# A transformer block on one core: the feed-forward's steps reordered within a slot, small columns given rings of their own, the last pair put first

## The chip, the cores and the metric

The kernel runs on one core of a Trainium2 chip. The core has a matrix engine (TensorE, "PE" in the profile, with its weight loads shown apart as "PEld"), a vector engine (VectorE, "DVE"), an activation engine (ScalarE, "ACT"), a general engine (GpSimd, "POOL") and a queue that here issues most transfers (SyncE, "SP"). Each works through its own instructions in order and they meet at semaphores. The metric is device time of one execution in microseconds (us); lower is better.

## What is computed

Sixteen sequences of 224 tokens with 512 features pass through a gated cross-attention and a gated feed-forward network with quantised activations and ternary weights. The context of a sequence has 750 rows, and a mask says which of them the softmax keeps. Cut to what matters:

```python
def xattn(x, context, mask):                       # 8 heads of 64
    q, k, v = x @ W_q, context @ W_k, context @ W_v          # split into heads
    sim = einsum('bihd,bjhd->bhij', q, k) * 64 ** -0.5
    sim = where(mask[:, None, None, :], sim, -finfo.max)
    return einsum('bhij,bjhd->bihd', softmax(sim), v).reshape(b, n, 512) @ W_o + b_o

def act_quant(x):                                  # to 8 bits, by row
    scale = 127.0 / clip(max(abs(x), axis=-1), 1e-5)
    return clip(round(x * scale), -128, 127) / scale

def weight_quant(w):                               # to -1, 0, 1
    scale = 1.0 / clip(mean(abs(w)), 1e-5)
    return clip(round(w * scale), -1, 1) / scale

def bitlinear(x, w, b):
    return einsum('bsd,fd->bsf', act_quant(rmsnorm(x)), weight_quant(w)) + b

def ffn(x):                                        # 512 -> 2048 -> 512
    return bitlinear(gelu(bitlinear(x, w1, b1)), w2, b2)

x = x + tanh(g_xattn) * xattn(layernorm(x), ctx, mask)
x = x + tanh(g_ffn) * ffn(layernorm(x))
```

## The kernel before, in words

**Two tilings.** Attention goes by *slots*: the 16 batches are sorted by how many context rows the mask leaves them, only those rows are gathered, and slot s handles the s-th batch with room for 192 rows (slots 0 to 7, called wide here) or 128 (slots 8 to 15, narrow). The feed-forward goes by *tiles* of 128 tokens, two of them making a *pair*: 28 tiles, 14 pairs. Tokens of all slots lie one after another, 224 to a slot, so a pair of 256 tokens begins in one slot and ends in the next.

**Attention of a slot.** `scores` (line 1037) makes one of four units of `sim`, takes off the mask's part and the row maximum on VectorE (L1061), the exponential on ScalarE (L1071), the reciprocal of the sum (`rec`, L1080), and multiplies the probabilities `p` by it on GpSimd (L1081). `turn_probs` (L1091) transposes them on TensorE (`ptp`, `ptr`), `weighted` (L1115) multiplies by the values (`av`) and stores the result transposed in `xoT`. Beside it run the steps for the next slot: `context_pieces` (`ctxp`, `kp`, `vp`, `vr`), `query_pieces` (`xnp`, `qp`) and `norm_pieces`.

**Feed-forward of a pair.**
- `residual(i)` (L1175) fetches the pair's rows of x into `y` by two indirect transfers on GpSimd's queue (L793) and adds the output bias there (L1182). `y` has three buffers.
- `project(i, k)` (L1184) multiplies `xoT` by `w_o` (`op`, L1189, eight matmuls for a tile as counted in the profile) and adds it to `y` on VectorE (L1192).
- `normalise(i)` (L1213) does layernorm and the first quantisation on VectorE, from the statistics (L1226) to the cast of `xq` (L1236), and transposes `xq` into `xqT` by a DMA from the SP queue (L1237). GpSimd works out the factor `c1` and adds the second bias to `y` (L1242 to L1247).
- `up(i, k, g)` (L1250) makes one half of the 2048 hidden columns of a tile (`hp`, L1259, eight matmuls) and evicts it with factor and bias on VectorE into `h` (L1267).
- `gelu(i, ks)` (L1272) applies the activation on ScalarE (L1279), takes the row's largest absolute value (L1282), quantises and casts to `hq` on VectorE (L1285, L1286), transposes it by a DMA from SP into `hqT` (L1288), and squares `h` on ScalarE for the row's norm (L1290), from which GpSimd makes the factor `c2` (L1292, L780, L1208 to L1210).
- `down(i, k)` (L1300) multiplies `hqT` by the second weights (`fp`, L1304, 16 matmuls), adds to `y` on VectorE (L1308), and scatters the tile to the output by an indirect transfer on GpSimd's queue (L1310).

**What sets the order.** In each slot the main loop (L1505 on) makes three streams: attention, the next slot's preparation, and `flow`, the feed-forward. Each is a list of pieces with a cost. `merge` (L1434) always takes the next piece of the stream that has done the smallest share of its own total cost, so a piece stands at a share of the slot. Before, `flow` is

```python
flow: residual(p); up(p-1), gelu(p-1); project(p), normalise(p); down(p-1)
```

`project` of a pair needs its 256 tokens complete, which holds in every slot from 2 on but slot 9. So slot 9 has only an up, slot 10 no up, slot 2 only a project. After the last slot come project and normalise of pair 13, up(12), then up(13) woven with down(12), then down(13).

The framework (Tile) is given this program order as priorities, and places each engine's instructions by a model of when their inputs are ready: an instruction that the model sees ready may go ahead of an earlier one that it sees waiting, and `tc.high_priority()` puts what is inside ahead of the rest. It also puts in all the waits, those for buffers among them. A tile's tag names its ring, and `bufs` how many buffers the ring has. Small columns of 2, 4 and 6 floats come from three rings (`small`, L782, of 24, 6 and 6 buffers), whatever they hold; `fx` of `normalise` and `hq` of `gelu` share a ring of three buffers. Results of TensorE wait for eviction in four small buffers (`gen`) and two of twice the size (`wide`, used by `sim`, `hp` and `av`).

Of the kernel before, what the change touches and what calls it, by code (L numbers as in the profile page):

```python
# [16 lines left out]
EPS = 1e-5  # L17
# [708 lines left out]
def compact_path(ctx, tc, sh, x, context, out, late_loads):  # L726
# [54 lines left out]

    def small(name, n=2):  # L782
        return pa.tile([P, n], F32, tag=f"s{n}", name=name, bufs=24 if n == 2 else 6)

# [159 lines left out]
    def norm(i, ks=(0, 1)):  # L944

        xp = normed[i]
        name = f"x{i}_{ks[0]}"
        part = slice(ks[0], ks[-1] + 1)
        mv = small(f"mv_{name}", 4).rearrange("p (k n) -> p k n", k=2)
        for k in ks:  # L950
            st = small(f"bs_{name}_{k}", 6)
# [3 lines left out]
        rstd = small(f"rs_{name}")  # L955
        nc.gpsimd.tensor_scalar(rstd[:, part], mv[:, part, 1], 1.0, EPS, ALU.mult, ALU.add)
        pow_half(rstd[:, part])
        less = small(f"ls_{name}")
        nc.gpsimd.tensor_scalar(less[:, part], mv[:, part, 0], -1.0, 0.0, ALU.mult, ALU.add)
        for k in ks:  # L960
            nc.gpsimd.tensor_scalar(
                xp[:, k, :], xp[:, k, :], less[:, k : k + 1], rstd[:, k : k + 1], ALU.add, ALU.mult
            )

    def norm_first(k):

        xp = normed[0]
        st = small(f"bs_x0_{k}", 6)
        nc.vector.bn_stats(st, xp[:, k, :])
        mv = small(f"mv_x0_{k}", 4)  # L970
        nc.vector.bn_aggr(mv[:, :2], st)
        rstd = small(f"rs_x0_{k}")
# [64 lines left out]
    def scores(s, n):  # L1037
# [16 lines left out]
        probs = pa.tile([TQ, 4, 192], F32, tag="p", name=f"p_{s}_{n}", bufs=3)  # L1054
        total = small(f"sum_{s}_{n}", 4)
        for i in range(2):
            for j in range(2):
# [20 lines left out]
                )  # L1078
        rec = small(f"rec_{s}_{n}", 4)
        nc.vector.reciprocal(rec[:TQ], total[:TQ])  # L1080
# [117 lines left out]
    def quantiser(amax, part, least, name):  # L1198
        k = small(f"k_{name}")
        nc.vector.tensor_scalar(k[:, part], amax[:, part], least, 1.0 / 127.0, ALU.max, ALU.mult)  # L1200
        nc.vector.reciprocal(k[:, part], k[:, part])
        load["v"] += 300
        return k

    def unquantiser(amax, r, part, isw, name):

        c = small(f"c_{name}")
        nc.gpsimd.tensor_tensor(c[:, part], amax[:, part], r[:, part], ALU.mult)  # L1208
        nc.gpsimd.tensor_scalar(c[:, part], c[:, part], 1e-5, None, ALU.max)
        nc.gpsimd.tensor_scalar(c[:, part], c[:, part], isw, None, ALU.mult)  # L1210
        return c

    def normalise(i, ks=(0, 1)):  # L1213
# [3 lines left out]
        part = slice(ks[0], ks[-1] + 1)  # L1217
        mv = small(f"mv_y{name}", 4).rearrange("p (k n) -> p k n", k=2)
        if ks[0] == 0:
            f["fx"] = late["rows"].tile([P, 2, D], F32, tag="hq", name=f"fx_{i}", bufs=3)  # L1220
            f["xq"] = pa.tile([P, 2, D], BF16, tag="xq", name=f"xq_{i}", bufs=3)
            f["xqT"] = pa.tile([P, 2 * ND, P], BF16, tag="xq", name=f"xqT_{i}", bufs=3)
        fx, xq, xqT = f["fx"], f["xq"], f["xqT"]
        for k in ks:
            st = small(f"bs_y{name}_{k}", 6)
# [3 lines left out]
        amax = small(f"a1_{name}")  # L1229
        nc.vector.tensor_reduce(amax[:, part], fx[:, part, :], AX.X, ALU.max, apply_absolute_value=True)  # L1230
# [9 lines left out]

        r = small(f"r1_{name}")
        nc.gpsimd.tensor_scalar(r[:, part], mv[:, part, 1], 1.0 + EPS, EPS * EPS, ALU.mult, ALU.add)  # L1242
# [29 lines left out]
    def gelu(i, ks=(0, 1)):  # L1272
        f = pairs[i]
        name = f"{i}_{ks[0]}"
        part = slice(ks[0], ks[-1] + 1)
        ss = small(f"ss_{name}")
        amax = small(f"a2_{name}")
        for k in ks:
            nc.scalar.activation(f["h", k], f["h", k], AF.Gelu)  # L1279
        for k in ks:  # L1280
            h = f["h", k]
            nc.vector.tensor_reduce(amax[:, k : k + 1], h, AX.X, ALU.max, apply_absolute_value=True)  # L1282
            scale = quantiser(amax, slice(k, k + 1), 1e-5 * EPS**0.5, f"2_{i}_{k}")
            hq = late["rows"].tile([P, FF], BF16, tag="hq", name=f"hq_{i}_{k}", bufs=3)
            nc.vector.tensor_scalar(hq.bitcast(I16), h, scale[:, k : k + 1], None, ALU.mult)  # L1285
            nc.vector.tensor_copy(hq, hq.bitcast(I16))  # L1286
# [4 lines left out]
        r = small(f"r2_{name}")  # L1291
        nc.gpsimd.tensor_scalar(r[:, part], ss[:, part], 1.0 / FF, EPS, ALU.mult, ALU.add)  # L1292
# [4 lines left out]
        load["v"] += len(ks) * (2282 + 1280 + 690)  # L1297
        load["s"] += len(ks) * 2 * 1910 + 2600

    def down(i, k):  # L1300
# [70 lines left out]
    def scale_weights(wi):  # L1371
        tot = small(f"wtot_{wi}")
# [3 lines left out]
        mean = small(f"wmean_{wi}")  # L1376
        nc.vector.tensor_scalar(mean[:, 0:1], pt, 1.0 / (FF * D), 1e-5, ALU.mult, ALU.max)
# [127 lines left out]
    for s in range(B):  # L1505
# [10 lines left out]
        else:  # L1516
# [4 lines left out]
            if complete:  # L1521
                flow.append((0.0, lambda i=projected: residual(i)))
            if raised < projected:
                flow += up_pieces(raised)
                raised += 1
            if complete:
                flow += project_pieces(projected)
                projected += 1
                if lowered < raised:
                    flow += down_pieces(lowered)  # L1530
                    lowered += 1
        merge(attention_pieces(s), other, flow)
# [8 lines left out]
    i = NPAIR - 1  # L1541
    residual(i)
    for k in range(2):
        project(i, k)
        normalise(i, (k,))
    downs = down_pieces(i - 1) + down_pieces(i)
    for _, piece in up_pieces(i - 1):
        piece()
    for _, piece in weave(up_pieces(i), downs[:2]) + downs[2:]:
        piece()  # L1550
# [34 lines left out]
```

## Time and profile before

| what | us |
|---|---|
| median of 6 runs (753.59 to 761.06) | 759.87 |
| the profiled execution | 759.97 |
| its span, first to last instruction | 758.1 |
| slots 3 to 7 (wide), 147.7 to 391.8 | 46.7 to 50.3 each |
| slots 8, 11 to 14, from one slot's first `sim` to the next | 39.2 to 40.9 each |
| slots 9 and 10 | 29.1 and 32.2 |
| slot 15, up to the first vector work on the last `op` | 653.55 to 692.85 |
| from there to the end of the span | 65.3 |

The profile shows one execution. An engine's busy time is the sum of what its instructions took. "A <- B" in the waits says that A's engine stood idle and what B it waited for last, with the total, the number of times and the longest. A line such as L1259 is a line of the kernel. The granted clock is the share of TensorE's full clock that the throttle allowed in a stretch. The weights of the feed-forward are loaded and rounded in slots 0 and 1, before any feed-forward work; the last `y` is followed by its transfer and the program's closing.

### The profile page before, as it was taken

The numbers are of one execution on the slowest core, as the hardware profiler recorded it, in microseconds if no ns is written. First come the engines' busy times: TensorE is split into PE (matmuls) and PEld (weight loads), VectorE is DVE, ScalarE is ACT, GpSimd is POOL, SyncE is SP. The second block draws the span as 40 slices with busy tenths as digits, with TensorE's granted clock in tenths as the row PEclk, the third lists the DMA queues.
The fourth block names the chain that finished last, engine by engine and source line by source line (L and its number), as shares of the span: only waits on it lengthen the run. The fifth ranks groups of instructions, "written<-read, shape, count | busy, mean of one in ns | idle before, by whom it ended". The sixth has DMA issues, their size and how long they took to land.

```text
span 758.1 us, 11378 instructions
## 1 busy us (share of the span) xinstructions
PE 685.4 (90%) x3902; PEld 437.1 (58%) x3902; DVE 505.6 (67%) x1300; ACT 407.7 (54%) x960; POOL 398.3 (53%) x543
## 2 busy tenths in 40 slices
PE   4997799999999999998999999999999999889652
PEld 3875587666566666555656575666666566443221
DVE  5499756876584674664758676588584939495860
ACT  1547565384663855736647368365565656460530
POOL 6583567464554644647266564575654454535141
PEclk9999899999999999999999999999999999999877
DMA  5884021132223322222142323123131222222250
GB/s 193 312 265 155 21 80 45 15 72 56 70 44 70 85 51 57 67 57 81 28 98 67 70 67 67 42 68 82 54 64 62 57 69 57 70 43 62 41 106 31
DMA packets 87218, 58.77 MB, mean 78 GB/s; under 512 B 75488, under 2 KB 75632, under 8 KB 87024
## 3 DMA queue, kind: packets, MB, share of 16 engines
q1 hardware_dynamic: 79024, 32.00, 18.8%
q0 software_dynamic: 8128, 25.96, 10.7%
q8 instruction: 33, 0.54, 0.3%
q14 instruction: 33, 0.27, 0.1%
HBM read 32.26 MB, written 7.34 MB: 52 GB/s over the span
## 4 chain that ended last, share of the span: by engine, by line
PE 58%; DVE 14%; issue 10%; POOL 9%; DMA 4%; ACT 3%; POOLq 0%; DVEq 0%; ACTq 0%; SPq 0%
PE qp L1008 9%; PE op L1189 9%; PE fp L1304 8%; PE hp L1259 7%; PE kp L892 5%; PE sim L1047 4%; PE vp L907 4%; PE ptp L1101 3%; DVE a L1282 3%; PE av L1126 3%; DVE h L1267 2%; POOL p L1081 2%; DMA hqT<-hq 2%; DVE hq L1285 2%; DVE p L1061 1%
## 5 line engine op out<-in xcount | busy, mean ns | idle before, releaser
L1081 POOL TENSOR_TENSOR p<-p,rec 112x768 f32<-112x768 f32 (+1 forms) x64 | 84.2, 1318 | 76.8 <-DVE rec L1080 43.9
L1304 PE MATMUL fp<-w2T,hqT 128*128 128x512 fp8e4 x448 | 106.7, 394 | 14.8 <-DMA hqT<-hq 14.8
L1259 PE MATMUL hp<-w1T,xqT 128*128 128x512 fp8e4 x448 | 107.4, 384 | 8.2 <-DVE h L1267 5.4
L1071 ACT ACTIVATE p<-p,nm 112x192 f32<-112x192 f32 (+1 forms) x256 | 106.4, 419 | 11.6 <-DVE nm L1061 11.4
L1008 PE MATMUL qp<-xnT,wq_sb 128*128 128x224 f32 x512 | 105.6, 360 | 0.6 <-ACT xnT L766 0.6
L1189 PE MATMUL op<-wo_sb,xoT 128*128 128x512 f32 x224 | 103.7, 599 | 0.0
L1008 PEld LDWEIGHTS qp<-xnT,wq_sb 128*128 128x128 f32 x512 | 97.4, 194 | 6.5 <-issue 3.6
L1267 DVE SCALAR_TENSOR_TENSOR h<-hp,c,b_bc 128x1024 f32<-128x1024 f32 x56 | 71.6, 1280 | 41.1 <-PE hp L1259 38.6
L1061 DVE CUSTOM_DVE_ANT_0 p<-sim,mask 112x192 f32<-112x192 f32 (+1 forms) x256 | 67.7, 319 | 34.2 <-PE sim L1047 32.7
L1304 PEld LDWEIGHTS <-hqT 128*128 128x128 bf16 x448 | 44.0, 101 | 73.6 <-DMA hqT<-hq 17.7
L1282 DVE TENSOR_REDUCE a<-h 128x1 f32<-128x2048 f32 x28 | 63.9, 2282 | 21.5 <-ACT h L1279 21.2
L1259 PEld LDWEIGHTS <-xqT 128*128 128x128 bf16 x448 | 43.5, 98 | 57.2 <-issue 15.2
L1308 DVE SCALAR_TENSOR_TENSOR y<-fp,c,y 128x512 f32<-128x512 f32 x28 | 20.9, 746 | 80.0 <-PE fp L1304 80.0
L1310 POOL DMA_INDIRECT out_dram<-y,token x28 | 30.9, 1104 | 78.2 <-DVE y L1308 74.0
L1290 ACT ACTIVATE h<-h 128x2048 f32<-128x2048 f32 x28 | 53.4, 1908 | 22.3 <-DVE hq L1285 14.9
L1279 ACT ACTIVATE h<-h 128x2048 f32<-128x2048 f32 x28 | 53.5, 1910 | 19.6 <-DVE k L1200 11.2
L1189 PEld LDWEIGHTS op<-wo_sb,xoT 128*128 128x128 f32 x224 | 40.6, 190 | 38.9 <-issue 36.4
L892 PE MATMUL kp<-ctxT,wk_sb 128*128 128x192 f32 (+1 forms) x384 | 63.0, 313 | 0.0
L892 PEld LDWEIGHTS kp<-ctxT,wk_sb 128*128 128x128 f32 x384 | 57.6, 198 | 6.4 <-issue 4.5
L1247 POOL TENSOR_TENSOR y<-y,b_bc 128x512 f32<-128x512 f32 x28 | 36.6, 1311 | 38.7 <-DVE fx L1228 38.4
L766 ACT COPY pT<-ptp 128x448 f32<-128x448 f32 x63 | 32.7, 536 | 40.3 <-PE ptp L1101 40.1
L1047 PE MATMUL sim<-kT,qT 64*112 64x192 f32 (+1 forms) x512 | 51.4, 316 | 1.1 <-DVE h L1267 1.0
(165 smaller groups left out, 1177.3 us busy)
## 6 DMA issues: line engine op xcount, KB each, us to landing
raw<-in_L_ffn_w_dram SPq DMA_DIRECT2D x16, 512.0 KB, 6.2
wq_sb<-in_L_xattn_W_q_dram SPq DMA_DIRECT2D x1, 1024.0 KB, 5.6
b_bc<-in_L_ffn_b_dram SPq DMA_DIRECT2D x1, 1024.0 KB, 9.5
wk_sb<-in_L_xattn_W_k_dram SPq DMA_DIRECT2D x1, 768.0 KB, 7.2
wv_sb<-in_L_xattn_W_v_dram SPq DMA_DIRECT2D x1, 768.0 KB, 8.6
wo_sb<-in_L_xattn_W_o_dram SPq DMA_DIRECT2D x1, 512.0 KB, 3.6
wo_sb<-in_L_xattn_W_o_dram SPq DMA_DIRECT2D x2, 256.0 KB, 6.6
x<-in_x_dram,token POOLq DMA_INDIRECT x28, 3.6
```

Of the source, the lines that this page charges most:

```text
L892: nc.tensor.matmul(pk[:, p - p0, :], lhsT=sh.wk[:, c, p * P : (p + 1) * P], rhs=st["ctxT"][:, c, :cap], start=(c == 0), stop=(c == NC - 1),)
L1008: nc.tensor.matmul(pq[:, i, :], lhsT=sh.wq[:, d, (p + i) * P : (p + i + 1) * P], rhs=st["xnT"][:, d, :], start=(d == 0), stop=(d == ND - 1),)
L1047: nc.tensor.matmul(sim[:, j, i, :cap], lhsT=st["qT"][j * DH : (j + 1) * DH, p, q * TQ : (q + 1) * TQ], rhs=st["kT"][j * DH : (j + 1) * DH, ...
L1061: nc.vector.tensor_tensor_reduce(out=probs[:, h, :cap], in0=sim[:, j, i, :cap], in1=st["mask"][:, j * begin : j * begin + cap], scale=-(DH ...
L1071: nc.scalar.activation(probs[:, h, :cap], probs[:, h, :cap], AF.Exp, bias=nmax, scale=-1.0, accum_out=total[:TQ, h : h + 1],)
L1081: nc.gpsimd.tensor_tensor(probs[:, :, :cap], probs[:, :, :cap], rec[:TQ].unsqueeze(2).to_broadcast([TQ, 4, cap]), ALU.mult,)
L1189: nc.tensor.matmul(po, lhsT=xoT[:, d, at : at + P], rhs=sh.wo[:, d, :], start=(d == 0), stop=(d == ND - 1))
L1259: nc.tensor.matmul(ph[:, n, :], lhsT=f["xqT"][:, k * ND + d, :], rhs=w1T[:, d, at : at + NB], start=(d == 0), stop=(d == ND - 1),)
L1267: nc.vector.scalar_tensor_tensor(h[:, cols], ph.rearrange("t i n -> t (i n)"), f["c1", k], sh.b1[:, cols], ALU.mult, ALU.add)
L1279: nc.scalar.activation(f["h", k], f["h", k], AF.Gelu)
L1282: nc.vector.tensor_reduce(amax[:, k : k + 1], h, AX.X, ALU.max, apply_absolute_value=True)
L1304: nc.tensor.matmul(po, lhsT=f["hqT", k][:, n, :], rhs=w2T[:, n, :], start=(n == 0), stop=(n == NF - 1))
```

## The change

1. **Order of a slot's flow.** It is now residual(p), project(p), normalise(p); down(p-1); up(p), gelu(p). A pair is raised in the slot that projects it, and lowered in the next one, ahead of that slot's up. Slot 9, with no project, now has only a down; slot 10 has no down; slot 2 has project and up of pair 0.
2. **After the last slot**, pair 13's project and normalise are traced inside `tc.high_priority()`; down(12) follows; then up(13), a half of the columns at a time, each half followed by its gelu and its reduce (`gelu_half`); then the quantisation, cast and transpose by halves (`quantise_halves`); then down(13). up(12) is no longer in this part.
3. **Small columns** have one ring of six buffers for each kind (`mvx`, `sum`, `k1`, `c2` and so on).
4. **`fx` and `hq`** have rings of their own, of one and two buffers.

The core of the diff:

```diff
-    def small(name, n=2):
-        return pa.tile([P, n], F32, tag=f"s{n}", name=name, bufs=24 if n == 2 else 6)
+    def small(kind, name, n=2):
+        return pa.tile([P, n], F32, tag=kind, name=f"{kind}_{name}", bufs=6)
...
-        total = small(f"sum_{s}_{n}", 4)
+        total = small("sum", f"{s}_{n}", 4)
...
-        k = small(f"k_{name}")
+        k = small("k" + name[0], name[2:])
...
-            f["fx"] = late["rows"].tile([P, 2, D], F32, tag="hq", name=f"fx_{i}", bufs=3)
+            f["fx"] = late["rows"].tile([P, 2, D], F32, tag="fx", name=f"fx_{i}", bufs=1)
...
-            hq = late["rows"].tile([P, FF], BF16, tag="hq", name=f"hq_{i}_{k}", bufs=3)
+            hq = late["rows"].tile([P, FF], BF16, tag="hq", name=f"hq_{i}_{k}", bufs=2)
...
+    def gelu_half(i, k, g):
+
+        f = pairs[i]
+        half = f["h", k][:, 2 * g * NB : 2 * (g + 1) * NB]
+        if g == 0:
+            f["a", k] = small("ah", f"{i}_{k}")
+        nc.scalar.activation(half, half, AF.Gelu)
+        nc.vector.tensor_reduce(f["a", k][:, g : g + 1], half, AX.X, ALU.max, apply_absolute_value=True)
+
+    def quantise_halves(i, k):
+        f = pairs[i]
+        h = f["h", k]
+        part = slice(k, k + 1)
+        amax = small("a2", f"{i}_{k}")
+        nc.vector.tensor_reduce(amax[:, part], f["a", k], AX.X, ALU.max)
+        scale = quantiser(amax, part, 1e-5 * EPS**0.5, f"2_{i}_{k}")
+        hq = late["rows"].tile([P, FF], BF16, tag="hq", name=f"hq_{i}_{k}", bufs=2)
+        f["hqT", k] = hqT = late["rows"].tile([P, NF, P], BF16, tag="hqT", name=f"hqT_{i}_{k}", bufs=2)
+        for g in range(2):
+            cols = slice(2 * g * NB, 2 * (g + 1) * NB)
+            nc.vector.tensor_scalar(hq.bitcast(I16)[:, cols], h[:, cols], scale[:, part], None, ALU.mult)
+            nc.vector.tensor_copy(hq[:, cols], hq.bitcast(I16)[:, cols])
+            nc.sync.dma_start_transpose(out=hqT[:, g * NF // 2 : (g + 1) * NF // 2, :], in_=hq[:, cols])
+        ss = small("ss", f"{i}_{k}")
+        nc.scalar.activation(h, h, AF.Square, accum_out=ss[:, part])
+        r = small("r2", f"{i}_{k}")
+        nc.gpsimd.tensor_scalar(r[:, part], ss[:, part], 1.0 / FF, EPS, ALU.mult, ALU.add)
+        pow_half(r[:, part])
+        f["c2", k] = unquantiser(amax, r, part, sh.isw[1], f"2_{i}_{k}")[:, part]
...
             if complete:
                 flow.append((0.0, lambda i=projected: residual(i)))
+                flow += project_pieces(projected)
+                projected += 1
+            if lowered < raised:
+                flow += down_pieces(lowered)
+                lowered += 1
             if raised < projected:
                 flow += up_pieces(raised)
                 raised += 1
-            if complete:
-                flow += project_pieces(projected)
-                projected += 1
-                if lowered < raised:
-                    flow += down_pieces(lowered)
-                    lowered += 1
...
     residual(i)
+    with tc.high_priority():
+        for k in range(2):
+            project(i, k)
+            normalise(i, (k,))
+    for _, piece in down_pieces(i - 1):
+        piece()
     for k in range(2):
-        project(i, k)
-        normalise(i, (k,))
-    downs = down_pieces(i - 1) + down_pieces(i)
-    for _, piece in up_pieces(i - 1):
-        piece()
-    for _, piece in weave(up_pieces(i), downs[:2]) + downs[2:]:
+        for g in range(2):
+            up(i, k, g)
+            gelu_half(i, k, g)
+        quantise_halves(i, k)
+    for _, piece in down_pieces(i):
         piece()
```

More of the change, by code (lines that the diff above doesn't have):

```diff
@@ L948, in norm @@
         part = slice(ks[0], ks[-1] + 1)
-        mv = small(f"mv_{name}", 4).rearrange("p (k n) -> p k n", k=2)
+        mv = small("mvx", name, 4).rearrange("p (k n) -> p k n", k=2)
         for k in ks:
-            st = small(f"bs_{name}_{k}", 6)
+            st = small("bsx", f"{name}_{k}", 6)
             nc.vector.bn_stats(st, xp[:, k, :])
@@ L954, in norm @@
             load["v"] += 850
-        rstd = small(f"rs_{name}")
+        rstd = small("rsx", name)
         nc.gpsimd.tensor_scalar(rstd[:, part], mv[:, part, 1], 1.0, EPS, ALU.mult, ALU.add)
         pow_half(rstd[:, part])
-        less = small(f"ls_{name}")
+        less = small("lsx", name)
         nc.gpsimd.tensor_scalar(less[:, part], mv[:, part, 0], -1.0, 0.0, ALU.mult, ALU.add)
@@ L967, in norm_first @@
         xp = normed[0]
-        st = small(f"bs_x0_{k}", 6)
+        st = small("bsx", f"x0_{k}", 6)
         nc.vector.bn_stats(st, xp[:, k, :])
-        mv = small(f"mv_x0_{k}", 4)
+        mv = small("mvx", f"x0_{k}", 4)
         nc.vector.bn_aggr(mv[:, :2], st)
-        rstd = small(f"rs_x0_{k}")
+        rstd = small("rsx", f"x0_{k}")
         nc.vector.tensor_scalar(rstd[:, :1], mv[:, 1:2], EPS, None, ALU.add)
@@ L1078, in scores @@
                 )
-        rec = small(f"rec_{s}_{n}", 4)
+        rec = small("rec", f"{s}_{n}", 4)
         nc.vector.reciprocal(rec[:TQ], total[:TQ])
@@ L1205, in unquantiser @@
     def unquantiser(amax, r, part, isw, name):
-        c = small(f"c_{name}")
+        c = small("c" + name[0], name[2:])
         nc.gpsimd.tensor_tensor(c[:, part], amax[:, part], r[:, part], ALU.mult)
@@ L1217, in normalise @@
         part = slice(ks[0], ks[-1] + 1)
[L1218 removed]
+        mv = small("mvy", name, 4).rearrange("p (k n) -> p k n", k=2)
         if ks[0] == 0:
[L1220 removed]
+            f["fx"] = late["rows"].tile([P, 2, D], F32, tag="fx", name=f"fx_{i}", bufs=1)
             f["xq"] = pa.tile([P, 2, D], BF16, tag="xq", name=f"xq_{i}", bufs=3)
@@ L1224, in normalise @@
         for k in ks:
-            st = small(f"bs_y{name}_{k}", 6)
+            st = small("bsy", f"{name}_{k}", 6)
             nc.vector.bn_stats(st, y[:, k, :])
@@ L1228, in normalise @@
             nc.vector.tensor_scalar(fx[:, k, :], y[:, k, :], mv[:, k, 0:1], None, ALU.subtract)
-        amax = small(f"a1_{name}")
+        amax = small("a1", name)
         nc.vector.tensor_reduce(amax[:, part], fx[:, part, :], AX.X, ALU.max, apply_absolute_value=True)
@@ L1239, in normalise @@
         )
-        r = small(f"r1_{name}")
+        r = small("r1", name)
         nc.gpsimd.tensor_scalar(r[:, part], mv[:, part, 1], 1.0 + EPS, EPS * EPS, ALU.mult, ALU.add)
@@ L1275, in gelu @@
         part = slice(ks[0], ks[-1] + 1)
-        ss = small(f"ss_{name}")
-        amax = small(f"a2_{name}")
+        ss = small("ss", name)
+        amax = small("a2", name)
         for k in ks:
@@ L1290, in gelu @@
             nc.scalar.activation(f["h", k], f["h", k], AF.Square, accum_out=ss[:, k : k + 1])
-        r = small(f"r2_{name}")
+        r = small("r2", name)
         nc.gpsimd.tensor_scalar(r[:, part], ss[:, part], 1.0 / FF, EPS, ALU.mult, ALU.add)
@@ L1371, in scale_weights @@
     def scale_weights(wi):
-        tot = small(f"wtot_{wi}")
+        tot = small("wtot", wi)
         nc.vector.tensor_reduce(tot[:, 0:1], weight_sums[wi], AX.X, ALU.add)
@@ L1375, in scale_weights @@
         nc.tensor.matmul(pt, lhsT=sh.ones, rhs=tot[:, 0:1], start=True, stop=True)
-        mean = small(f"wmean_{wi}")
+        mean = small("wmean", wi)
         nc.vector.tensor_scalar(mean[:, 0:1], pt, 1.0 / (FF * D), 1e-5, ALU.mult, ALU.max)
```

## The prediction

> **What bounds the kernel now.** I read four views: the page's busy rows, busy time by stage, the list of waits, and the timeline of the end. A "slot" is one batch's step; it begins with the `sim` matmuls of that batch, and slot 15, the last, begins at 653.55 us.
>
> First, the page, in 40 slices of 19 us:
>
> ```profile
> PE 685.4 (90%) x3902; PEld 437.1 (58%) x3902; DVE 505.6 (67%) x1300; ACT 407.7 (54%) x960; POOL 398.3 (53%) x543
> PE   4997799999999999998999999999999999889652
> DVE  5499756876584674664758676588584939495860
> PEclk9999899999999999999999999999999999999877
> ```
>
> PE is full from slice 7 to slice 34, and in the last four slices it falls to 9652. So the middle can only win back small gaps; the end has room. Second, busy time of each engine in slots 3 to 14, slot 14, slot 15, and two stretches of the end (columns: length, PE, weight loads, DVE, ACT, POOL, clock, DMA):
>
> ```profile
> 147.70:653.55 505.85, 491.21 (x2767) 309.65 (x2765) 340.25 (x876) 297.56 (x700) 270.57 (x370) 0.99 0.27 64
> 614.40:653.55 39.15, 39.03 (x215) 24.51 (x214) 27.30 (x67) 22.54 (x54) 18.61 (x27) 1.00 0.26 61
> 653.55:692.80 39.25, 32.72 (x154) 15.82 (x154) 25.93 (x66) 20.02 (x47) 19.54 (x27) 0.96 0.29 67
> 692.80:733.70 40.90, 27.33 (x105) 11.04 (x103) 36.10 (x48) 15.37 (x12) 13.43 (x29) 0.86 0.27 55
> 733.70:758.10 24.40, 8.71 (x32) 3.45 (x32) 1.50 (x2) 1.34 (x2) 3.56 (x7) 0.71 0.21 52
> ```
>
> Slots 3 to 14 leave PE 505.85 - 491.21 = 14.6 us idle. From 692.80 to 733.70 DVE is busy 36.1 of 40.9: there the feed-forward's vector work is the limit, with PE at 27.3. Third, the waits:
>
> ```profile
> PE ptp L1101 <- POOL p L1081: 16.0, 11, 4.0
> PE fp L1304 <- DMA hqT<-hq: 14.8, 5, 9.3
> POOL y L793 <- DMA out_dram<-y,token: 22.6, 11, 2.3
> ```
>
> The transposes of probabilities wait for POOL (about 10.3 of those 16.0 us fall in slots 3 to 14); `fp`, the down projection, waits at the end for its transposed input. Fourth, the end (start, length, engine, what; in brackets the idle time before it):
>
> ```profile
> 675.83 3.63 PE L1304 MATMUL fp<-w2T,hqT 128*128 128x512 fp8e4 x16 [1.43 <-DMA hqT<-hq]
> 714.34 5.80 PE L1304 MATMUL fp<-w2T,hqT 128*128 128x512 fp8e4 x16 [0.62 <-DMA hqT<-hq]
> 732.98 0.69 DVE L1286 CAST hq<-hq 128x2048 bf16<-128x2048 int16 x1
> 735.92 8.71 PE L1304 MATMUL fp<-w2T,hqT 128*128 128x512 fp8e4 x32 [9.31 <-DMA hqT<-hq]
> 744.73 0.75 DVE L1308 SCALAR_TENSOR_TENSOR y<-fp,c,y 128x512 f32<-128x512 f32 x1 [2.70 <-PE fp L1304]
> ```
>
> The last cast ends at 733.67; 11.06 us later the last `y` is formed.
>
> **The change, part by part.** The sum is made against the profiled execution, 759.97 us (span 758.1), which is within 0.1 us of the median, 759.87.
>
> *Order of a slot.* Before, slot s does up(p-1), project(p), down(p-1); after, project(p), down(p-1), up(p). Through slot 14 the old kernel has raised pairs 0 to 10, the new one 0 to 11: one up more, in slot 2, while slots 9 and 10 exchange an up for a down. One up is four groups of eight matmuls with 1.73 us from start to start: **+6.9 us** of PE before slot 15, which PE, full there, can't hide. In return up(11), its gelu and most of its vector work have left slot 15.
>
> *Stalls in slots 3 to 14.* The merge gives each piece a share of the slot. The flow costs 2 x 1.8 + 2 x 3.5 + 4 x 1.8 = 17.8. Attention's first probability transposes stand at share 0.24 of a narrow slot. Before them the flow had three up groups (5.2 us); now it has both projects and one down (2 x 3.45 + 3.46 = 10.4 us). POOL gets 5 us more to finish `p`, about the longest stall (4.0). The scores at 0.32 and their transposes at 0.63 move the other way: between them lay two projects and a down (10.4 us), now a down and an up group (5.2 us). That distance, 12 to 17 us, becomes 7 to 12, and the units took 8.8 us in slot 14 (`sim` at 614.36, second `p` done 623.2), part of it behind the residual fetch's POOL wait. That wait (2.0 us in slot 14) moves too: out rows now leave in mid slot, the fetch that reuses their buffer follows them, and behind it on POOL stand the second units' `p`. I take 5 of the 10.3 us as gone and 2 as new: **-3**. The ends are -10 (nearly all idle time of slots 3 to 14) and +3 (the 10.3 us back at the second transposes, with a third more); the first half of the slot moves by more than the longest wait, the second half keeps its distance only just, so I stay near the middle.
>
> *up behind its own pair's normalisation.* In slot 6 `y` of the second project was ready at 323.6 and the cast of `xq` ended at 334.3, 10.7 us; the transpose takes 3.1 (median row; 4.6 at most). So 13.8 to 15.3 us, against (0.60 - 0.20) x 39.8 = 15.9 us of slot between the second project and the first up in a narrow slot, more in slots 3 to 7 (47 to 50 us long). I cost it at nothing; the cover is two downs and the score work. If the cover is late by x, each slot pays x: rival 1. Slots 2 and 10 have no down between; the scheduler can place other ready matmuls there.
>
> *down one slot later.* Its hqT, of the previous slot's end, is due 8 to 16 us into the slot. From the last up group: eviction 1.28, gelu 1.91, reduce 2.28, quantise 2.3, transpose 4.3 = 12.1 us. The first tile is a quarter slot earlier still. Nothing. The gelu of the second tile now stands ahead of the next exponentials on ACT with its 1.28 us table load; ACT is busy 22.5 of 39.15 us, and the first transposes have the 5 us to cover it. Nothing.
>
> *Slot 15 and the end.* DVE's work from 653.55 to the last cast is 25.93 + 36.10 = 62.0 us in 80.1, so 18.1 idle. The new slot 15 lacks up(11)'s four evictions (5.1), one reduce (2.28), one quantiser and quantisation (2.3): -9.7. Halves add per tile one reduce (2 x 1.22 - 2.28 = 0.16), one cast (2 x 0.43 - 0.69 = 0.17), a combining reduce and a second quantise start (0.2): 1.1 for two. Work 53.4. Idle I build from the new chain: 4 while up(12) waits for its own xqT (transpose 3.1, first group's lead), 3.3 for its second group and the gelu (1.4 + 1.9), 3 for the half gelus of the last pair, 2.2 for crossings: 12.5. Ends: 7.5 (the first two alone) and 18.1 (as before). Slot 15 starts at 653.55 + 6.9 - 3 = 657.45, the last cast ends at 657.45 + 53.4 + 12.5 = 723.4, **10.3 earlier** than 733.67.
>
> *Urgent last pair.* Its normalisation already runs as soon as `op` is there (692.85 on DVE); put first it displaces, but adds no work. 0, inside the idle range.
>
> *Last half.* After the last cast only a 128x1024 transpose (the size of an xqT, 3.1) and eight matmuls (half of 5.80) remain, plus 0.5 to the eviction: 6.5 in place of 11.06, **-4.6**. Ends: 9.9 if the first half's transpose delays it (the longest hqT took 7.0, + 2.9), 4.2 (2.4 + 1.8).
>
> *Small columns and fx/hq.* No line of the waits names a small column as a ring's holder, and two hq plus one fx hold what three shared slots held. Six buffers cover three pairs at two a pair. 0; it can cost at most what it lets the scheduler reorder, which the body's range covers.
>
> Sum: -10.3 - 4.6 = -14.9, so 759.97 - 14.9 = **745 us**.
>
> A rule that speaks against it: the section "What's actually happening" in the Trainium skill's "TensorE: Matmul & The Clock Gate" says that an idle window of about 3.4 us puts the matmul clock back to half. The trace shows the like: 16 `fp` matmuls took 3.63 us at 675.83 and 5.80 at 714.34, granted clock 0.86 and then 0.71. An estimate by that page is 1.7 us lost per restart, by the rows 2.2. With three more gaps in a thinner end that is 5 or 7 us of PE time, most of it where DVE sets the pace; charged in full it would make 750 or 752.
>
> **The rivals.**
>
> 1. *up waits in every slot (slower).* In-order PE stands at `hp` for xqT. For it: 13.8 to 15.3 us of need against 15.9. Against: DVE idles 12 of 39 us in slot 14, and wide slots have slack. At 2.2 us in each of 12 slots: 745 + 26 = 771. It decides from 14.9 / 12 = 1.2 us per slot on.
> 2. *The end stays as idle as it was (no change).* The urgent pair pushes up(12)'s gelu back, idle stays 18.1 (+5.6), transposes queue (+3.4), and the body's stalls come back (+6): 760.
> 3. *Only the body disappoints.* Stalls +3 in place of -3: 751. For it: the POOL wait only moves.
> 4. *The order isn't taken.* The scheduler keeps up behind other work, and slot 15 still holds it: the extra up returns, only the halves stay, 760 - 4.6 = 755.
>
> **How the numbers follow.** A measurement of this kernel can tell about 0.5%, 3.8 us. Forecast with rival 3: 0.58. Rival 4: 0.12. Rival 2: 0.10. Rival 1: 0.20. Faster by more than 0.5% (below 756): the forecast, and rival 4: 0.70. Within: 0.08, most of rival 2. Slower: rival 1 and the rest of 2, 0.22. The forecast's own range: best 653.55 + 6.9 - 10 + 53.4 + 7.5 = 711.4, 22.3 earlier, and 6.9 off the last half: 731; worst, with body and idle at their bad ends and the last half as taken, 653.55 + 6.9 + 3 + 53.4 + 18.1 = 734.95, 1.3 later, less 4.6: 757. The range for 8 in 10 leaves out the combination of all best ends and the upper half of rival 1: 734 to 767.
>
> **What would show it.** Slot 15's `sim` near 657; after it no `hp` of pair 11, and the first matmuls `op`. The wait of `ptp` for POOL at slot starts gone. Between the last cast and the last `y` 6 to 7 us. DVE's idle time from slot 15's start to the last cast under 18. Wrong if PE's idle before `hp` names xqT's transpose in most slots, or if PE idle in slots 3 to 14 exceeds 20 us.

## The result, and the profile after

The changed kernel is slower: 762.19 us (median of 23 runs, 758.7 to 770.19) against 756.48 us for the kernel before on the same chips (49 runs), a ratio of **1.0092** with a 95% interval of 1.0068 to 1.0117. A second series gave 1.0094 (1.0061 to 1.0128). Forecast were 745 us, a ratio of 0.980. The profiled execution took 771.63 us (span 769.9); a second profile of the same kernel (767.69, span 765.9) has the same shape and is used where a sum is made. Of the 23 runs 13 took 758.7 to 763.35 us and 10 took 766.47 to 770.19, and both profiled executions are of the longer kind, so sums on them show more loss than the medians do (5.7 us).

Below line 1299 the new code is 30 lines longer, so `fp` is L1334 here, its eviction L1338, and the halves are L1306 to L1321. The slices of the changed kernel's page, each a fortieth of the span:

```profile
PE   4989899899999999998999979889999999997852
DVE  4588766566693866839559464586494949496970
PEclk9969999999999999999999989998999999999986
```

The end is not thinner than before (7852 against 9652), but the body, formerly full, has holes at slices 24, 26 and 27. Slots 3 to 14, slot 14, slot 15 to the last cast, and the rest (columns as before: length, PE, weight loads, DVE, ACT, POOL, clock, DMA):

```profile
158.80:678.60 519.80, 495.18 (x2767) 311.77 (x2765) 346.47 (x874) 280.85 (x685) 269.10 (x364) 0.98 0.27 62
637.40:678.60 41.20, 39.14 (x215) 24.27 (x214) 29.27 (x68) 22.56 (x54) 18.76 (x27) 1.00 0.24 58
678.60:747.69 69.09, 55.64 (x238) 24.89 (x238) 57.85 (x116) 32.30 (x58) 27.84 (x52) 0.93 0.28 58
747.69:769.90 22.21, 6.16 (x21) 2.11 (x19) 1.50 (x2) 1.49 (x2) 3.58 (x7) 0.73 0.26 63
```

PE idles 519.80 - 495.18 = 24.6 us in slots 3 to 14, where it idled 14.6. From slot 15's first `sim` to the last cast DVE is busy 57.85 of 69.09 us; before it was 62.02 of 80.12. PE's waits, in total, times, longest:

```profile
PE fp L1334 <- DMA hqT<-hq: 10.8, 4, 6.1
PE sim L1047 <- DVE nm L1061: 6.9, 4, 2.8
PE op L1189 <- DVE keys L833: 6.5, 4, 1.8
PE hp L1259 <- DMA xqT<-xq: 5.4, 4, 2.4
PE ptp L1101 <- POOL p L1081: 2.7, 3, 1.9
```

The wait of the probabilities' transposes for POOL has gone as foretold, 16.0 to 2.7 us. In its place stand waits of `sim` and of the second `op` for the vector engine, at the start of a slot, and of `hp` for its own pair's transpose, mostly in slots 2 and 10 (2.40 and 1.92 us). The 24.6 us pass the 20 that the prediction had named as a sign of being wrong. The end:

```profile
738.96 9.70 PE L1334 MATMUL fp<-w2T,hqT 128*128 128x512 fp8e4 x32 [6.06 <-DMA hqT<-hq]
747.12 0.57 DVE L1321 CAST hq<-hq 128x1024 bf16<-128x1024 int16 x1
751.35 5.19 PE L1334 MATMUL fp<-w2T,hqT 128*128 128x512 fp8e4 x16 [2.69 <-DMA hqT<-hq]
756.64 0.75 DVE L1338 SCALAR_TENSOR_TENSOR y<-fp,c,y 128x512 f32<-128x512 f32 x1 [7.12 <-PE fp L1334]
```

From the end of the last cast, 747.69, to the last `y` it is 8.95 us, where it was 11.06. So the end is better and the body is worse. By the second profile: slot 15's first `sim` starts at 674.41, 20.9 us later than before; from there to the last cast 69.1 us in place of 80.1 (-11.0); from the cast to the last `y` 8.95 in place of 11.06 (-2.1). Sum +7.8, which is the difference of the spans, 765.9 - 758.1.

### The profile page after: what moved, and what is told of

Same layout as the page of the kernel before. It is cut to its first block, busy times and chain, and to the rows that moved or that the text cites. A ratio compares the mean times of both kernels' runs of the same rounds, so it can differ in the third digit from the quotient of the medians.

```text
span 769.9 us, 11356 instructions
## 1 busy us (share of the span) xinstructions
PE 694.7 (90%) x3902; PEld 441.4 (57%) x3902; DVE 512.0 (67%) x1304; ACT 394.5 (51%) x954; POOL 393.4 (51%) x543
## 4 chain that ended last, share of the span: by engine, by line
PE 61%; DVE 19%; DMA 6%; ACT 5%; issue 3%; POOL 1%; DVEq 0%; POOLq 0%; ACTq 0%; SPq 0%
PE qp L1008 11%; PE fp L1334 11%; PE hp L1259 11%; PE op L1189 8%; PE kp L892 4%; PE av L1126 3%; PE vp L907 3%; DVE a L1282 3%; PE ptp L1101 2%; PE sim L1047 2%; DMA raw<-in_L_ffn_w_dram 2%; ACT h L1279 2%; DVE hq L1285 2%; DVE h L1267 2%; PE vr L918 1%
## 5 line engine op out<-in xcount | busy, mean ns | idle before, releaser
L1334 PE MATMUL fp<-w2T,hqT 128*128 128x512 fp8e4 x448 | 109.8, 402 | 16.4 <-DMA hqT<-hq 10.8
L1189 PE MATMUL op<-wo_sb,xoT 128*128 128x512 f32 x224 | 111.1, 638 | 8.6 <-DVE keys L833 6.5
L1334 PEld LDWEIGHTS <-hqT 128*128 128x128 bf16 x448 | 45.1, 102 | 73.8 <-issue 16.1
L1061 DVE CUSTOM_DVE_ANT_0 p<-sim,mask 112x192 f32<-112x192 f32 (+1 forms) x256 | 70.1, 315 | 16.8 <-PE sim L1047 13.2
L1189 PEld LDWEIGHTS op<-wo_sb,xoT 128*128 128x128 f32 x224 | 42.9, 202 | 54.9 <-issue 42.5
L1282 DVE TENSOR_REDUCE a<-h 128x1 f32<-128x2048 f32 x26 | 59.4, 2283 | 18.3 <-ACT h L1279 18.3
L1292 POOL TENSOR_SCALAR r<-ss 128x1 f32<-128x1 f32 x26 | 5.0, 190 | 118.8 <-ACT h L1290 117.8
L1279 ACT ACTIVATE h<-h 128x2048 f32<-128x2048 f32 x26 | 49.6, 1908 | 26.7 <-DVE h L1267 26.7
L1290 ACT ACTIVATE h<-h 128x2048 f32<-128x2048 f32 x26 | 49.7, 1910 | 25.1 <-DVE hq L1285 21.3
L1047 PEld LDWEIGHTS sim<-kT,qT 64*112 64x112 f32 x512 | 38.2, 176 | 24.8 <-DVE nm L1061 9.2
L766 ACT COPY qT<-qp 128x448 f32<-128x448 f32 x30 | 15.8, 528 | 65.7 <-PE qp L1008 65.7
```

The source lines that it names most:

```text
L1047: nc.tensor.matmul(sim[:, j, i, :cap], lhsT=st["qT"][j * DH : (j + 1) * DH, p, q * TQ : (q + 1) * TQ], rhs=st["kT"][j * DH : (j + 1) * DH, ...
L1061: nc.vector.tensor_tensor_reduce(out=probs[:, h, :cap], in0=sim[:, j, i, :cap], in1=st["mask"][:, j * begin : j * begin + cap], scale=-(DH ...
L1189: nc.tensor.matmul(po, lhsT=xoT[:, d, at : at + P], rhs=sh.wo[:, d, :], start=(d == 0), stop=(d == ND - 1))
L1334: nc.tensor.matmul(po, lhsT=f["hqT", k][:, n, :], rhs=w2T[:, n, :], start=(n == 0), stop=(n == NF - 1))
```

## The experiments

Each ratio is to the kernel before on the same chip, with its 95% interval. "End" is the time from the end of slot 15's last `av` to the end of the span (before: 682.2 to 758.1, 75.9 us).

### The parts alone

First the changed kernel once more, and its three parts by themselves: the rings in the old order and with the old end; the new order alone, whose end is only `down(12)`, `up(13)` whole, `down(13)`; and the new end alone in the old order.

> The whole change once more, for a trace of its more frequent course. Theory A (the new order gathers vector work at the start of a slot, so that the matrix engine waits for evictions there): matrix engine idle in slots 3 to 14 well above the 14.6 us of before, about 25, and slot 15 beginning 14 us or more after 653.55; time 0.4 to 1.5% above the kernel before. Theory B (the rings of small columns): the same time, no prediction on where.

> Only the rings by kind, and fx and hq in rings of their own; the order of slots and the end as before. Theory A: the same time as before within 0.3%. Theory B: it carries the loss, 0.5 to 1% slower.

> Only the new order in a slot (project, down, up); rings as before; after the last slot project and normalise, down(12), up(13) whole, down(13), nothing urgent, no halves. Theory A: slots 2 to 14 lose what they lose in the whole change (slot 15 begins 14 to 25 us after 653.55), the end wins some 10, the time is 0.5 to 1.5% above the kernel before. Theory B: slot 15 begins near 657, as forecast, and the time is about 1.5% below before.

The edit in the main loop (the part after the last slot is left out here):

```diff
             if complete:
                 flow.append((0.0, lambda i=projected: residual(i)))
+                flow += project_pieces(projected)
+                projected += 1
+            if lowered < raised:
+                flow += down_pieces(lowered)
+                lowered += 1
             if raised < projected:
                 flow += up_pieces(raised)
                 raised += 1
-            if complete:
-                flow += project_pieces(projected)
-                projected += 1
-                if lowered < raised:
-                    flow += down_pieces(lowered)
-                    lowered += 1
```

> Only the end: the order in the slots and the rings as before; pair 13 urgent, its gelu, reduce, quantisation and transpose by halves; up(12) still after the last slot. Theory A: slots 2 to 14 as before, the last cast to the last y 6 to 8 us in place of 11.06, so 2 to 5 us (0.3 to 0.6%) faster. Theory B: the same.

Measured: whole 1.0094 (1.0061 to 1.0128); rings alone **1.0372** (1.0328 to 1.0417); order alone 1.0047 (1.0018 to 1.0076); end alone 0.9967 (0.9932 to 1.0002). What I had costed at nothing is the dearest part by itself, dearer than either theory allowed (1% at most). The parts don't add: together they cost far less than the rings alone. The order alone came out near the low end of theory A (slot 15 begins at 667.13, 13.6 us later; end 66.7), and so did the end alone. In the rings' profile one wait is new: the vector engine stands 40.9 us in 15 places before the first `bn_stats` of an x fetch (L952), where it never stood before (total, times, longest).

```profile
DVE bsx_x L952 <- DMA x<-in_x_dram,token: 40.9, 15, 8.8
```

Hence the next question, which ring.

### Which ring: the statistics of x

> The kernel before with one edit: the statistics of an x fetch (bs of 6 columns, mv of 4) take rings of their own, six buffers each, in place of the rings that they shared with those of y, the sums and the reciprocals. Theory T1, the shared rings held these statistics back until the fetch had landed: the vector engine now reaches them too early and stands before them about 40 us in all, as it did with all rings by kind (40.9 us); ratio to before 1.02 to 1.04. Theory T2, the loss of the rings by kind comes from the two-column ring or from fx and hq: stands under 8 us there, ratio 0.995 to 1.005.

```diff
...
-        mv = small(f"mv_{name}", 4).rearrange("p (k n) -> p k n", k=2)
+        mv = small(f"mv_{name}", 4, "mvx").rearrange("p (k n) -> p k n", k=2)
...
-            st = small(f"bs_{name}_{k}", 6)
+            st = small(f"bs_{name}_{k}", 6, "bsx")
...
```

> The complement, in the order and with the end of before: two-column values in rings by kind, fx and hq apart, but everything of four and six columns in its old shared ring. T1: ratio 0.995 to 1.010, and the vector engine waits for an x fetch under 8 us in all. T2: ratio 1.025 to 1.04. If both share the loss: 1.01 to 1.025.

Measured: with only these two rings split **1.0265** (1.0234 to 1.0296), and PE's order of work is almost unchanged. With only the two-column rings split, and `fx` and `hq` apart, everything of four and six columns shared, 1.0087 (1.0056 to 1.0119), with no wait at L952. Its profile has slot 15's `av` 4.2 us earlier than before and the old end 3 us longer (78.8), but as its span is shorter than before's (756.9 for 758.1), it doesn't show where the 0.9% goes. T1 holds for the larger part. The kernel with the two rings split has this among the vector engine's waits (total, times, longest):

```profile
DVE bs_x L952 <- DMA x<-in_x_dram,token: 43.2, 15, 8.2
```

and in its timeline this in slot 8 (GpSimd's issues, the vector engine, PE; start, length, idle time before it in brackets):

```profile
394.92 1.07 POOL L793 DMA_INDIRECT y<-in_x_dram,token  x1 [2.00 <-DMA out_dram<-y,token]
403.30 1.03 POOL L793 DMA_INDIRECT x<-in_x_dram,token  x1 [0.16 <-issue]
404.63 1.00 POOL L793 DMA_INDIRECT x<-in_x_dram,token  x1 [0.31 <-issue]
407.08 0.70 DVE L952 BATCH_NORM_STATS2 bs_x<-x 128x6 f32<-128x512 f32 x1 [8.16 <-DMA x<-in_x_dram,token]
414.65 0.78 PE L1047 MATMUL sim<-kT,qT 64*112 64x128 f32 x8 [3.88 <-DVE h L1267]
```

The vector engine stood at the statistics from 398.92, over 4 us before GpSimd even issued the fetch: that queue was behind a `y` fetch which waited for an output row, the bias, and a `p`. Behind the vector engine stood the evictions of `h`, and for one of those PE. In the kernel before the fetch is issued at the same place, but the statistics ran 18 us later:

```profile
402.07 1.04 POOL L793 DMA_INDIRECT x<-in_x_dram,token  x1 [0.16 <-issue]
419.89 0.68 DVE L952 BATCH_NORM_STATS2 bs_x<-x 128x6 f32<-128x512 f32 x1
```

The same three slots (8, 9 and 11, from one slot's last `av` to the next; columns as above), of before and then with the two rings split:

```profile
384.00:426.70 42.70, 40.18 (x228) 24.74 (x225) 31.34 (x83) 24.64 (x57) 28.18 (x43) 1.00 0.33 81
426.70:460.80 34.10, 32.27 (x196) 20.88 (x196) 19.45 (x57) 22.51 (x55) 17.81 (x24) 1.00 0.30 68
491.30:528.70 37.40, 36.40 (x210) 23.24 (x209) 31.21 (x77) 23.30 (x56) 24.14 (x34) 1.00 0.30 76
```

```profile
384.80:433.50 48.70, 41.84 (x224) 25.38 (x225) 30.44 (x81) 24.45 (x57) 28.22 (x48) 0.96 0.30 70
433.50:474.40 40.90, 35.14 (x196) 22.36 (x196) 19.33 (x59) 22.74 (x55) 17.01 (x20) 0.92 0.21 57
505.20:548.60 43.40, 39.46 (x209) 24.59 (x209) 30.00 (x77) 23.08 (x56) 21.26 (x33) 0.92 0.28 65
```

With the two rings split PE idles 6.86, 5.76 and 3.94 us in them (2.52, 1.83 and 1.00 before), its clock is 0.96, 0.92 and 0.92, and nearly the same matmuls take it 41.84, 35.14 and 39.46 us. So of 18.8 us lost in three slots 11.2 are waits and 7.6 a slower clock behind them.

So the shared rings had been a brake. I take the mechanism to be this: Tile hands the buffers of one ring out in the program's order, so a column of x that stands behind others in its ring can't be taken before them. The runs show the effect; for the reason there is one further sign, that the programs with the shared rings enlarged (from 6 to 24 buffers, or from 24 to 48) have the same instructions in the same order on every engine, the waits left aside. So it is the sharing, not the number of buffers, that sets the order; no program with enlarged rings was timed.

### The whole change without the rings of four and six columns, and without any

> The whole change without its rings (all small columns, fx and hq as before): the new order of a slot, the urgent last pair, its gelu by halves. If the parts add, the order's 1.0047 and the end's 0.9967 make 0.998 to 1.003. If the end's gain is lost in the new order, or the rings cost nothing there: 1.005 to 1.012, as with the whole change (1.0092). The body ends 12 to 15 us later than before in slot 14 by either theory.

> The whole change, with the four- and six-column statistics back in their shared rings, two-column values by kind, fx and hq apart. T1: the 7 us that the rings added between slots 2 and 14 go, ratio 0.998 to 1.004, the same as without any of the rings. T2, the two-column rings or fx and hq carry them: 1.007 to 1.012.

```diff
-        return pa.tile([P, n], F32, tag=kind, name=f"{kind}_{name}", bufs=6)
+        return pa.tile([P, n], F32, tag=f"s{n}" if n > 2 else kind, name=f"{kind}_{name}", bufs=6)
```

Measured: with everything of four and six columns shared again **1.0020** (0.9995 to 1.0046). (I call this kernel "x statistics shared"; the statistics of `y`, the sums and the reciprocals went back with those of x.) So these rings together make 0.7% of the whole change, its whole loss to within the error. How much of it is due to the two rings of x alone was not measured in the new order; there the vector engine's wait at L952 is 6.7 us in five places with the rings split, and none with them shared. But with none of the new rings the ratio is 1.0128 (1.0092 to 1.0164), slower than anything foreseen: the body is the same (slot 15's `av` ends at 695.2 in both), the end is 70.0 us against 59.9. Some other ring of the change is worth ten microseconds. All rings together are thus not dearer than none (1.0094 and 1.0128, with intervals that overlap).

### What the other rings are good for

> The new order and the new end with one thing of the rings: fx and hq apart; all small columns as before. It stands between order_and_tail (ratio 1.0128, end from slot 15's last av 70.0 us) and the whole change with the x statistics shared (1.002, end 59.9). Theory F, the urgent pair's fx took the third slot of the shared ring and the next hq had to wait: 1.000 to 1.004, end 58 to 62. Theory G, the two-column rings made the difference: 1.010 to 1.015, end near 70.

> The old order of a slot with the new end (urgent, halves, 0.9967 by itself) and fx and hq apart; all small columns as before. Theory F: the end gains as it does in the new order, 71.8 us becomes 62 to 67, ratio 0.985 to 0.992. Theory G: 0.995 to 1.000.

Measured: fx and hq apart, 1.0094 (1.0058 to 1.0130), end 70.2; in the old order 0.9994 (0.9967 to 1.0020), end 71.5. Theory F falls: it isn't fx and hq. The next two take the two-column rings.

> The new order, the new end, fx and hq apart (ratio 1.0094, end 70.2 us after slot 15's last av) with one edit: the four small columns of the last pair's normalise take a ring of their own; all others share theirs as before. Theory R, a shared ring hands its buffers out in the program's order, so that the urgent columns stood behind those of the gelu before: the wait of 9.2 us in front of the second tile's fp(12) goes or moves behind up(13), end 59 to 62, ratio 0.998 to 1.003. Rival, the other rings by kind did it: end near 70, ratio 1.007 to 1.012.

```diff
-        return pa.tile([P, n], F32, tag=f"s{n}", name=f"{kind}_{name}", bufs=24 if n == 2 else 6)
+        return pa.tile([P, n], F32, tag=f"s{n}" + "last" * (kind in ("a1", "k1", "r1", "c1") and name[:3] == "13_"), name=f"{kind}_{name}", bufs=24 if n == 2 else 6)
```

> The whole change with the x statistics shared (ratio 1.002, end 59.9), without the urgent last pair: its projection and normalise have the program's own place. Theory R: the vector engine's order of the end is again that of the shared ring, end 68 to 72, ratio 1.008 to 1.014. The prediction's step, urgency is worth nothing: end 59 to 62, ratio 1.000 to 1.004.

```diff
-    with tc.high_priority():
-        for k in range(2):
-            project(i, k)
-            normalise(i, (k,))
+    for k in range(2):
+        project(i, k)
+        normalise(i, (k,))
```

Measured: last pair's columns apart **1.0028** (0.9997 to 1.0058), end 62.6. Without urgency 1.0074 (1.0045 to 1.0103), end 65.5. From the timeline of the end (vector engine and PE) with the columns shared, fx and hq apart:

```profile
704.31 0.49 DVE L1228 TENSOR_SCALAR fx<-y,mvy 128x512 f32<-128x512 f32 x1
715.40 0.68 DVE L1230 TENSOR_REDUCE a<-fx 128x1 f32<-128x512 f32 x1
719.91 5.87 PE L1334 MATMUL fp<-w2T,hqT 128*128 128x512 fp8e4 x16 [9.23 <-DMA hqT<-hq]
725.61 7.07 PE L1259 MATMUL hp<-w1T,xqT 128*128 128x512 fp8e4 x32
```

and with the last pair's own ring:

```profile
703.46 0.49 DVE L1228 TENSOR_SCALAR fx<-y,mvy 128x512 f32<-128x512 f32 x1
703.98 0.69 DVE L1230 TENSOR_REDUCE a<-fx 128x1 f32<-128x512 f32 x1
710.14 3.63 PE L1259 MATMUL hp<-w1T,xqT 128*128 128x512 fp8e4 x16 [0.33 <-DMA xqT<-xq]
722.96 5.31 PE L1334 MATMUL fp<-w2T,hqT 128*128 128x512 fp8e4 x16 [4.10 <-DMA hqT<-hq]
```

In the first, `fx` of pair 13 is ready at 704.80, but the reduction of it, whose result is a small column, starts 10.6 us later: the columns of up(12)'s second gelu come first in their ring. So up(13) can't fill PE's wait for hqT. In the second the reduction follows within 0.03 us, and up(13) runs 15 us earlier. Theory R holds for the last pair; urgent and a ring of its own belong together: with urgency alone the end is 70.2 us, with the rings alone 65.5, with both 62.6 or 59.9. The order alone, with neither and without halves, had 66.7, so urgency and halves without the ring gained nothing there. The run without urgency lies between both forecasts (65.5 us, for 68 to 72 or 59 to 62).

### What is left in the body

PE's idle time by slot, from one slot's last `av` to the next (us), before and with the x statistics shared:

| slot | 2 | 3 | 4 | 5 | 6 | 7 | 8 | 9 | 10 | 11 | 12 | 13 | 14 |
|---|---|---|---|---|---|---|---|---|---|---|---|---|---|
| before | 0.1 | 0.0 | 2.0 | 1.3 | 1.9 | 3.7 | 2.5 | 1.8 | 0.0 | 1.0 | 0.1 | 0.1 | 0.1 |
| new order | 3.4 | 1.6 | 1.6 | 1.8 | 1.8 | 2.5 | 0.0 | 3.9 | 2.5 | 0.3 | 0.8 | 1.2 | 1.2 |

The new order wins 4 us in slots 4 to 8, where I had looked for it, and loses elsewhere: +7.9 us over slots 2 to 14. Slots 2 and 10 are the ones with no down between a projection and the up behind it, and there `hp` waits for xqT, 2.0 and 2.5 us. Slot 9 has only a down. One run takes the down from slot 9 and puts it into slot 10.

> The whole change with the x statistics shared, and down(6) moved from slot 9 to slot 10, between the projection of pair 7 and its up. Theory W, up waits for its own pair's normalise where no down lies between: PE's 2.5 us before hp in slot 10 go and the idle time of slots 9 and 10 together, 6.5 us, falls to 2 to 4; ratio 0.996 to 1.002. Rival, the idle time of these slots belongs to the vector engine's load: 6 to 8 us stay, ratio 1.001 to 1.006.

```diff
-            if lowered < raised:
+            if lowered < raised and s != 9:
```

Measured 1.0045 (1.0013 to 1.0077). Slot 10 has no idle time left, so the cause there is named rightly, but slot 9 now idles 6.25 us at a clock of 0.84. Together 6.25 against 6.47: the gap only moves, and the rival's numbers hold. In slots 12 to 14 the named wait is `op` for ScalarE's `ctxT` (2.5 us in two places); I made no run on it.

### A version that is faster than both

> A combination: the old order through slot 13, up(11) added to the end of slot 14's flow, the new order in slot 15 alone; end and rings of the whole change, x statistics shared. If the new order's loss lies in the slots before 14 (7.1 us more PE idle there, and 6.9 of the extra up which stays): slot 14's av at 653 to 656, the end 60 as in the new order, ratio 0.990 to 0.996. If it lies in the extra up and what follows it, or if the end needs the new order throughout: 1.000 to 1.005.

Against the old order, cut to the main loop:

```diff
 # old order: up(p-1), project(p), down(p-1); then, new:
-            if raised < projected:
+            if raised < projected and s < B - 1:
                 flow += up_pieces(raised)
                 raised += 1
 ...
+            if s >= B - 2:
+                flow += up_pieces(raised)
+                raised += 1
```

> The old order in every slot with up(12) added to the flow of slot 15 (up(11), op(12), down(11), up(12)); end and rings as in the run with the switch in slot 14. PE is 30 of 35 us busy in slot 15, the vector engine 24, so its 6.9 us are partly hidden: slot 15's av at 683 to 688, the end 60 to 66 as the vector engine has up(12)'s work anyway: ratio 0.985 to 0.997. If the vector engine is full there, the end stays at 72: 1.000 to 1.008.

> The combination with the switch of order in slot 14 (ratio 0.9934, end 60.1), its rings by kind taken out again but for the last pair's four columns; fx and hq apart. If the last pair's columns are all that the rings are good for: 0.990 to 0.997, end 59 to 62. If the rings by kind carry more: 0.998 to 1.005.

> The same kernel as the combination with the switch of order in slot 14, run again: 0.990 to 0.997 if its gain is real; 0.998 to 1.003 if the first measurement was lucky.

> That combination with the last pair's gelu whole in place of halves. The prediction's term says that the halves save 4.6 us after the last cast: ratio to before 1.000 to 1.003 if the combination itself is at 0.9934, the time from the last cast to the last y 10 to 11.5 us in place of 7.2. If the halves only shift work on the vector engine: 0.990 to 0.996.

Measured: switch in slot 14 **0.9934** (0.9905 to 0.9963), and again **0.9907** (0.9872 to 0.9941), 750.31 us beside 757.51. It pays the extra up once and late, keeps the body of before, and has the new end (60.1 us). In slot 15 instead 1.0060 (1.0032 to 1.0088), a clear miss: its profile has

```profile
694.09 6.04 PE L1259 MATMUL hp<-w1T,xqT 128*128 128x512 fp8e4 x16 [6.73 <-DMA xqT<-xq]
```

and slot 15 lasts 53.4 us in place of 34.7. That is the wait of rival 1, met in the last slot, which has little else to place there; 6.7 of the 18.7 us, the rest being mostly the up itself at a lower clock. The shorter form with only the last pair's ring measured 1.0011 (0.9979 to 1.0043), as forecast if the other two-column rings carry more; its end is near (62.3), but slots 8 and 14 are 2.3 and 3.3 us longer. Why isn't shown. With the gelu whole 0.9945 (0.9917 to 0.9973). The last cast, the last 16 `fp` and the last `y` in the timeline of the repeat, with halves:

```profile
728.35 0.57 DVE L1321 CAST hq<-hq 128x1024 bf16<-128x1024 int16 x1
732.59 3.63 PE L1334 MATMUL fp<-w2T,hqT 128*128 128x512 fp8e4 x16 [2.69 <-DMA hqT<-hq]
736.32 0.75 DVE L1338 SCALAR_TENSOR_TENSOR y<-fp,c,y 128x512 f32<-128x512 f32 x1 [5.57 <-PE fp L1334]
```

and with the gelu whole:

```profile
730.57 0.69 DVE L1286 CAST hq<-hq 128x2048 bf16<-128x2048 int16 x1
736.63 5.86 PE L1334 MATMUL fp<-w2T,hqT 128*128 128x512 fp8e4 x16 [4.78 <-DMA hqT<-hq]
742.60 0.75 DVE L1338 SCALAR_TENSOR_TENSOR y<-fp,c,y 128x512 f32<-128x512 f32 x1 [9.89 <-PE fp L1334]
```

7.40 and 11.34 us from the end of the cast: in these two executions the halves save 3.9 us there, 1.7 of them in the wait and 2.2 in the matmuls. The two ratios, 0.9907 and 0.9945, differ by 2.9 us, within their intervals. Taken alone 0.9945 lies in the range forecast for halves that only shift work; the switch itself came out lower than that forecast assumed, so the whole time doesn't settle what the halves are worth.

## Why the prediction was wrong

The forecast's parts were +3.9 us to slot 15, -14.2 from there to the last cast, -4.6 behind it. The second profile has +20.9, -11.0 and -2.1. Of the 22.7 us between the two sums, 17.0 lie in the body, 3.2 before the last cast, 2.5 behind it. So what failed is the body, and in it two terms, the rings at nothing and the stalls at -3. With the x statistics shared slot 15 begins at 665.04, 7.6 us after the 657.45 forecast; the other 9.4 us came with the rings of four and six columns (674.41), in the profiles. The ratios put these rings at 5.6 us, and without them the change still gains nothing (1.0020).

- **Small columns and fx/hq, 0: the first step that failed.** "It can cost at most what it lets the scheduler reorder" was true, but I took the body's range for the bound of that without looking at what the rings kept in place. The two rings of x cost 2.65% alone in the old order (20 us); all rings of four and six columns cost 0.7% (5.6 us) in the new. The two-column rings, above all the last pair's, work the other way, with ten microseconds at the end, which the forecast had counted among its gains without naming what they need. That all rings together come near nothing is luck, two large effects of opposite sign.
- **Urgent last pair, 0: wrong too, the other way.** It is worth 4.1 us (1.0074 against 1.0020), and only as the last pair's columns no longer share their ring; with them shared the end is 70 us.
- **Stalls in slots 3 to 14, -3: the second step that failed, wrong in sign.** Even with the x statistics shared they grew by 4.5 us (14.65 to 19.18), and slot 2 adds 3.3, past the bad end of the term, +3. The POOL wait went as argued, and slots 4 to 8 gained 4; what I had not costed is slots 2 and 10, where an up is left with nothing in front of it ("the scheduler can place other ready matmuls there" was the failing phrase), slot 9 with its down alone (4 us), and the vector engine's load at a slot's start.
- **One up more, +6.9: right.** With the x statistics shared PE is busy 39.27 us in slot 2, before 32.80, 6.5 more.
- **up behind its own pair's normalise, 0: right in the slots with a down.** The 5.4 us in four waits fall in slots 2 and 10 (4.3) and in the end (1.0); rival 1 at 2.2 us in each of 12 slots did not come. The need was also read too high: the second `op` of slot 6 ends at about 323.7, but its `y` only at 325.06, so from `y` to the cast it is 9.2 us, not 10.7.
- **Slot 15 and the end.** The idle time was right, 69.09 - 57.85 = 11.2 for 12.5. The vector work was mis-sized: 57.85 for 53.4. up(11) was less far along when slot 15 began than I had taken: in the profile of the change its last eviction (679.50), a reduction (683.81) and most of two quantisations with their casts fall behind 678.60. I had let all four evictions leave and all but one reduction and quantisation; what stayed beyond that is about 3 of the 4.4 us.
- **Last half, -4.6: right in kind.** It is -2.1 in the changed kernel, and -3.9 with halves and whole gelu compared. I had left eight matmuls behind the last cast; all 16 of the last tile stand there, from 3.66 us after the cast and 5.19 us long (751.35), so the bad end that I had named (9.9) was nearer.
- **The clock.** I named the rule and put it into no term. (The clocks given with its two rows, 0.86 and 0.71, are those of the last two stretches; the row at 714.34 lies in the first of these.) The trace of the changed kernel shows it act in slot 11: behind a gap of 2.84 us the 8 matmuls of an `op` took 6.49 us, at a granted clock of 0.55, where others took 3.60.

```profile
476.18 3.60 PE L1189 MATMUL op<-wo_sb,xoT 128*128 128x512 f32 x8
519.50 0.77 PE L1047 MATMUL sim<-kT,qT 64*112 64x128 f32 x2 [2.84 <-DVE nm L1061]
520.19 6.49 PE L1189 MATMUL op<-wo_sb,xoT 128*128 128x512 f32 x8
```

"What's actually happening" in the Trainium skill's "TensorE: Matmul & The Clock Gate" states a window of about 3.4 us of idleness before the clock halves. The ratio 1.80 agrees with a halving, while the one gap in these records is shorter than the window.

The rivals: none had the sign for the right reason. Rival 3 named the right place, the body, with stalls of +3 us where they grew by 10.0 (24.6 for 14.6). Rival 2's price (760) is near the time measured, but its story is not what happened in the changed kernel, whose end did gain 13 us; it is what happened without the rings, where slot 15's start to the last cast took 79.2 us, for 80.1 before.

## What to carry to other kernels

A ring that unlike values share is also an order: it can hold back work whose input is late, and it can hold up work that was made urgent. Before splitting one, list what each value stands behind, and above all which reads a transfer that the schedule may believe to be there; after splitting, look for one new wait of an in-order engine on a DMA. And a reordering that helps at the end of a program can be made there alone: with the switch in slot 14 and the x statistics shared the kernel gained 0.7 to 0.9%, where the change as a whole lost 0.9%.

## What the hardware showed that was not expected

- The vector engine's standing still cost PE more than PE's waits: with the two rings of x split, 11.2 us of idle time in three slots came with 7.6 us of slower matmuls, at granted clocks of 0.92 to 0.96.
- In the same run the vector engine stood 8.16 us for a fetch that takes a median of 3.6 us from issue to landing. Most of it was the issue, which came 4.4 us late because GpSimd's queue was behind another fetch and its waits.
